# Denominators of 352 channels inverted by GpSimd as a power of minus one

## The chip, the cores and the metric

One core of a Trainium2 chip. The time is device microseconds from launch to end of one execution; where several runs were made, their median is given.

## The reference, cut to what matters

The input is 8 x 1024 tokens of 256 numbers. The first layer is an attention inside each token: its 16 heads have 64 channels, and channel q of a head attends to the channels k up to q of the same head, with one number each for query, key and value.

```python
Q = (x @ Wq + bq).reshape(b, s, H, C) * inv_sqrt_c      # H = 16, C = 64
K = (x @ Wk + bk).reshape(b, s, H, C)
V = (x @ Wv + bv).reshape(b, s, H, C)
scores = jnp.einsum('bshq,bshk->bshqk', Q, K)
scores = jnp.where(mask, -inf, scores)                  # k > q is masked
w = jax.nn.softmax(scores, axis=-1)
attn = jnp.einsum('bshqk,bshk->bshq', w, V).reshape(b, s, H * C)
x = _layernorm(x + attn @ Wo + bo)
```

So each token has 1024 sums of exponentials (denominators) and 1024 weighted sums (numerators), one pair for each channel. The rest of the reference is a second layer (attention over 8 tokens, then a mixture of eight experts) and is not touched by the change.

## The kernel before, in words

`phase_a` computes the first attention, `phase_b` and `phase_c` the second layer. `phase_a` works in 64 tiles of 128 tokens (t) and in each through eight parts (c = 0 to 7); a part is four heads of 64 tokens. The order of the work is written out by hand (`tc.manual_schedule()`): the loop over t and c at the end of `phase_a` calls the steps of a part, and the lists `fill_a`, `middle`, `between` and `fill_b` say which other steps go between them. A sign says for which tile: "" this one, "+" the next, "-" the one before. Each engine executes its instructions in the order in which this loop issued them; an instruction that waits holds up all that is behind it on its engine.

The channels have two ways. Of the 1024 channels, columns 0 to 351 and 672 to 1023 go wholly through TensorE. For the 320 columns between them (`own`), part of the pairs is computed on the token layout by VectorE, GpSimd and ScalarE (`token_scores` L583, `token_less` L591, `token_exp`, `token_weigh` L607 and L616, `token_sums` L625) and added by `complete` (L631, L637).

The TensorE way, for each part:

- `build` (L394, L400) copies queries and keys into the layouts R and L by DMA: four copies of R and two of L are issued by GpSimd, the other copies of L by SP. There are two sets of R and L, used in turn, each for two parts.
- `gather` (L408) is a memset of one number on GpSimd that waits for these copies; the matmuls of the scores wait for it.
- `scores` (L433, L443) makes the scores in PSUM, and ScalarE their exponentials (L458).
- `sums` (L481) makes numerators and denominators, and ScalarE copies them to S (L502). There are two buffers of S, one for the even and one for the odd pair of parts.
- `bring_back` (L521, L522), once for two parts, copies them from S to `nd`, by five DMAs that GpSimd issues. `nd` is [128 tokens, 2, 1024]: numerators and denominators. There is one buffer of it for all tiles.

After the last part of a tile its `nd` is divided while the next tile runs: `invert` (L644) makes reciprocals of the denominators, `divide` (L648) multiplies them with the numerators, both in three pieces of columns: 0 is 0 to 351, 1 is the 320 in the middle, 2 is 672 to 1023. `turn` (L657) transposes the result, `output` (L686) multiplies it by Wo, and `norm_scalars` and `normal` make the layer norm; `norm_scalars` (L76, L79) adds the epsilon to the variance and raises it to the power -0.5 on GpSimd, one column at a time.

Around the change the steps are as follows. `bring_back` of the parts c = 0 and 1 is called at c = 3 (`fill_a`), of c = 2 and 3 at c = 4 (`fill_b`), that of the others as soon as they are done. It overwrites the `nd` of the tile before, so that the steps that read it are issued first: `invert` 0 and 2 at c = 0, `complete` at c = 1, `invert` 1 and the three `divide` at c = 2. At c = 3 and 4 the projections of the next tile's query and value (L355, L322) also go through one PSUM bank (`ps`), which VectorE empties (L356, L329); `products` (L377, L378) are two multiplications on GpSimd, at c = 2 and c = 4, behind VectorE's work (`behind`).

Of the kernel before, what the change touches and what calls it, by code (L numbers as in the profile page):

```python
# [24 lines left out]
FP = mybir.dt.float32  # L25
# [4 lines left out]
ALU = mybir.AluOpType  # L30
# [3 lines left out]
P = 128  # L34
# [18 lines left out]
def fused_kernel(ctx: ExitStack, tc: tile.TileContext, a: dict, out: bass.AP):  # L53
# [68 lines left out]
    ]  # L122

    phase_a(tc, a, ident, x1_d, norm_scalars, share, view)

    late = ctx.enter_context(tc.tile_pool(name="late", bufs=1))
# [39 lines left out]
def phase_a(tc, a, ident, x1_d, norm_scalars, share, view):  # L166
# [8 lines left out]
    nc = tc.nc  # L175
    G = 4
    NR = 4
    T0, TC = 352, 320
# [24 lines left out]
    with (  # L203
# [83 lines left out]
        event = wp.tile([1, 1], FP, name="event")  # L287
        wait = mybir.DependencyInfo(mybir.DependencyClass.Sync, mybir.DependencyReason.DATA)
        nd = wp.tile([P, 2, HID], FP, name="nd")
        Ss = [wp.tile([P, 4, 2 * G, C1], FP, name=f"S{i}") for i in range(2)]  # L290
        nc.gpsimd.memset(Ss[0][:, :, 2 * G - 2 :, 0:32], 0.0)
        nc.gpsimd.memset(Ss[1][:, :, :3, 0:32], 0.0)
# [3 lines left out]
        state = {}  # L296
# [330 lines left out]
        columns = (slice(0, T0), own, slice(T0 + TC, HID))  # L627
# [10 lines left out]
                )  # L638

        def invert(t, n):  # L640
            if n == 0:
                state["att", t] = op.tile([P, HID], FP, name="att")
            cols = columns[n]
            nc.vector.reciprocal(state["att", t][:, cols], nd[:, 1, cols])  # L644

        def divide(t, n):
# [149 lines left out]
        def lead_v(k):  # L796
            xT = view["xT"].rearrange("p c b l n -> p c b (l n)")
            ps = pq.tile([P, 2, 512], FP, name="pair")
            for b in range(2):
# [40 lines left out]
        fill_a = {  # L840
            0: [("", spread_v, 1, 0), ("", spread_v, 1, 1)],
            2: [("-", residual)],
            3: [("", bring_back)],
            5: [
                ("+", maxima, 1), ("", token_weigh, "D"), ("+", token_scores, "F"),
                ("", token_less, "C"), ("-", residual_bias),
# [10 lines left out]
        fill_b = {  # L857
            0: [
                ("", token_less, "F"), ("", token_less, "B"),
                ("-", invert, 0), ("-", invert, 2), ("+", extrema, 0),  # L860
            ],
            1: [("-", complete), ("", token_weigh, "A"), ("", token_scores, "D")],
            2: [
                ("+", products, 0), ("", token_less, "D"),
                ("-", invert, 1), ("", token_sums, "A"), ("-", divide, 0), ("-", divide, 1), ("-", divide, 2),
            ],
            3: [("", token_scores, "C"), ("+", maxima, 0), ("+", extrema, 1), ("", token_weigh, "F")],
            4: [
                ("-", turn), ("+", products, 1), ("", bring_back),
                ("", token_sums, "F"), ("", token_weigh, "B"),  # L870
# [924 lines left out]
```

## Time and profile before

| | |
|---|---|
| median of 2 runs | 4562.82 us (4562.46 to 4563.17) |
| profiled execution, its own time | 4519.66 us |
| its span (first to last instruction) | 4517.9 us |
| clock granted to TensorE, mean | 0.981 |
| TensorE, matmuls | 4306.8 us busy, 95% |
| TensorE, weight loads (beside matmuls) | 2921.1 us, 65% |
| VectorE | 3884.2 us, 86% |
| ScalarE | 3511.9 us, 78% |
| GpSimd | 2958.0 us, 65% |
| `phase_a` | to about 3,800 us of the span |
| reciprocals, L644 | 192 on VectorE, 430.1 us in all |

The page names the engines PE (TensorE; PEld its weight loads), DVE (VectorE), ACT (ScalarE), POOL (GpSimd) and SP. Busy shares are over the whole span. Durations and positions come from the one profiled execution, whose time is 43.2 us (0.9%) below the median of the runs. In a group's line the number after x is the count of instructions, then busy us and mean ns of one, then the idle time of the engine before them and what ended it. In a timeline a line begins with start and duration in us; like instructions in a row are put together. Spans on GpSimd are rough.

### The profile page before, as it was taken

How to read it: one execution, taken by the hardware profiler on the slowest of the kernel's cores; microseconds unless marked ns; L12 is line 12 of the kernel's file. 1: busy time of each engine (PE TensorE's matmuls, PEld its weight loads, DVE VectorE, ACT ScalarE, POOL GpSimd, SP SyncE). 2: the span in 40 equal slices, each digit the busy share in tenths (PEclk: the TensorE clock that was granted, in tenths of full speed). 3: DMA queues.
4: the chain of work that ended last, by engine and by line, in shares of the span. 5: the costliest groups of instructions: out<-in, count | busy, mean ns of one | idle time of the engine just before them, and what ended most of it. 6: DMA issues, size and time to landing. Idle time of an engine off the chain costs nothing. (4 is left out here: it accounts for less than half of the span.)

```text
span 4517.9 us, 164489 instructions
## 1 busy us (share of the span) xinstructions
PE 4306.8 (95%) x68440; PEld 2921.1 (65%) x68440; DVE 3884.2 (86%) x6686; ACT 3511.9 (78%) x5271; POOL 2958.0 (65%) x4391
## 2 busy tenths in 40 slices
PE   7999999999999999999999999999999997888695
PEld 4666666666666666666666666666666665555473
DVE  6889888998888888988998889888888884677778
ACT  5888888888888888888888888888888884444244
POOL 6777777777777777777777777777777772233456
PEclk9999999999999999999999999999999998999897
DMA  2222222222222222222222222222222222232553
GB/s 83 52 54 56 53 54 53 56 54 56 54 53 56 55 56 54 55 55 55 53 56 52 55 54 56 54 56 52 55 55 56 55 53 76 53 76 73 144 167 113
DMA packets 449603, 285.64 MB, mean 63 GB/s; under 512 B 324314, under 2 KB 390234, under 8 KB 448854
## 3 DMA queue, kind: packets, MB, share of 16 engines
q0 software_dynamic: 102368, 164.18, 13.3%
q1 hardware_dynamic: 343718, 109.03, 12.0%
q8 instruction: 536, 8.78, 0.8%
q10 hardware_dynamic: 2768, 1.91, 0.2%
q14 instruction: 213, 1.74, 0.1%
HBM read 72.84 MB, written 33.85 MB: 24 GB/s over the span
## 5 line engine op out<-in xcount | busy, mean ns | idle before, releaser
L458 ACT ACTIVATE e<-pair 128x1024 f32<-128x1024 f32 (+1 forms) x2560 | 2377.1, 983 | 462.2 <-PE pair L443 444.5
L443 PE MATMUL pair<-R,L 32*128 32x128 f32 (+1 forms) x27648 | 1375.4, 321 | 11.9 <-ACT e L458 9.5
L481 PE MATMUL sum<-e,V 128*32 128x256 f32 (+1 forms) x27648 | 1270.5, 320 | 12.2 <-ACT S L502 4.0
L443 PEld LDWEIGHTS pair<-R,L 32*128 32x128 f32 x27648 | 1059.4, 186 | 172.2 <-issue 123.7
L481 PEld LDWEIGHTS sum<-e,V 128*32 128x32 f32 x27648 | 747.4, 110 | 523.0 <-ACT e L458 116.4
L591 POOL TENSOR_TENSOR s<-s,qm 128x1280 f32<-128x1280 f32 (+2 forms) x320 | 596.2, 1888 | 208.6 <-DVE s L583 124.6
L521 POOL DMA_DIRECT2D nd<-S x1024 | 513.9, 509 | 275.2 <-ACT S L502 274.7
L344 DVE COPY V<-vT 32x128 f32<-32x128 f32 (+2 forms) x2048 | 450.9, 220 | 188.9 <-PE sum L481 162.8
L394 POOL DMA_DIRECT2D R<-qm x1024 | 519.6, 522 | 100.5 <-PE pair L443 89.3
L502 ACT COPY S<-sum 128x512 f32<-128x512 f32 (+2 forms) x1152 | 545.8, 488 | 10.6 <-PE sum L481 4.4
L377 POOL TENSOR_TENSOR qm<-qm 128x512 f32<-128x512 f32 x128 | 162.7, 1271 | 487.0 <-DVE qm L356 401.7
L644 DVE RECIPROCAL att<-nd 128x352 f32<-128x352 f32 (+1 forms) x192 | 430.1, 2264 | 1.6 <-DMA nd<-S 1.4
L433 PE MATMUL pair<-late,sel 32*128 32x256 bf16 (+2 forms) x5120 | 385.6, 286 | 3.6 <-ACT e L458 3.6
L616 DVE TENSOR_TENSOR s<-s,vt 128x1280 f32<-128x1280 f32 (+2 forms) x320 | 363.9, 1152 | 6.6
L607 DVE TENSOR_REDUCE part<-s 128x80 f32<-128x1280 f32 (+3 forms) x320 | 358.9, 1137 | 10.2 <-ACT s L598 10.2
L583 DVE TENSOR_TENSOR s<-k,qm 128x1280 f32<-128x1280 f32 (+2 forms) x320 | 363.6, 1153 | 0.1
L625 DVE TENSOR_REDUCE part<-s 128x80 f32<-128x1280 f32 (+3 forms) x320 | 357.5, 1132 | 2.2
L400 POOL DMA_DIRECT2D L<-k x511 | 332.7, 660 | 7.1 <-issue 6.8
L598 ACT ACTIVATE s<-s 128x1280 f32<-128x1280 f32 (+1 forms) x256 | 312.7, 1221 | 8.4 <-POOL s L591 8.4
L76 POOL TENSOR_SCALAR ve<-mv 128x1 f32<-128x1 f32 x128 | 101.5, 793 | 326.5 <-DVE mv L74 300.6
L322 PEld LDWEIGHTS ps<-xT,wv 128*128 128x128 f32 x2048 | 238.3, 192 | 44.3 <-issue 41.8
L433 PEld LDWEIGHTS <-sel 32*128 32x128 bf16 x5120 | 136.2, 92 | 202.1 <-issue 191.8
(259 smaller groups left out, 5708.1 us busy)
## 6 DMA issues: line engine op xcount, KB each, us to landing
R<-qm POOLq DMA_DIRECT2D x1024, 64.0 KB, 2.4
L<-k SPq DMA_DIRECT2D x3577, 8.0 KB
nd<-S POOLq DMA_DIRECT2D x1024, 32.0 KB, 2.0
nd<-S POOLq DMA_DIRECT2D x256, 128.0 KB, 2.6
rows_d<-yx SPq DMA_DIRECT2D x32, 512.0 KB
xT<-in_xT SPq DMA_DIRECT2D x64, 128.0 KB
xr<-in_x SPq DMA_DIRECT2D x64, 128.0 KB
x_d<-x1o SPq DMA_DIRECT2D x64, 128.0 KB
```

Source lines behind the costliest of these rows:

```text
L344: nc.vector.tensor_copy(V[32 * aa : 32 * aa + 32, :, :, aa, 0:4], src[32 * qd : 32 * qd + 32, :n, ww, :, aa, :],)
L394: moved.append((None, nc.gpsimd.dma_start(R[:, b, b, :], q[:, b, :, cols])))
L433: nc.tensor.matmul(bank[u][:, a0:a1].rearrange("p (n i) -> p n i", i=n)[:, :, 0:32], sel[pr].rearrange("p a j -> p (a j)"), late[pr, None, ...
L443: one = nc.tensor.matmul(bank[u][:, starts[h] : starts[h] + 4 * m].rearrange("p (b i) -> p b i", i=m), Lt[pr, 2 * (h0 + h) + jb].rearrange ...
L458: nc.scalar.activation(es[i][:, :, :at], pair[i][:, :, :at], AF.Exp)
L481: nc.tensor.matmul(dst[32 * u : 32 * u + 32, :, width - n :], Vs[ww][:, H1 * jb + v, u, :], e[u // 2][:, u % 2, starts[h] : starts[h] + 4 ...
L502: nc.scalar.copy(S[:, :, to + x : to + x + nh, C1 - width :].rearrange("p b h i -> p h b i"), ps[:, start : start + 4 * nh * width].rearra ...
L521: nc.gpsimd.dma_start(tok[:, b, 0, cols], Sx[:, b, b, :])
L583: shared(nc.vector.tensor_tensor(s, k, q, ALU.mult))
L591: one = nc.gpsimd.tensor_tensor(s, s, m, ALU.subtract)
L616: shared(nc.vector.tensor_tensor(to, s, v, ALU.mult))
L644: nc.vector.reciprocal(state["att", t][:, cols], nd[:, 1, cols])
```

## The change

The reciprocals of columns 0 to 351 (`invert` 0) are made on GpSimd, as the denominators raised to a power that is a constant column of minus one, broadcast over 352 columns. They are issued at c = 3 (`fill_a`) instead of c = 0. The pieces 1 and 2 stay reciprocals on VectorE, where they were. `divide` 0 moves from c = 2 to the start of `fill_b` at c = 3, and the `bring_back` that stood at c = 3 in `fill_a` now follows it.

```diff
         nd = wp.tile([P, 2, HID], FP, name="nd")
+        minus_one = wp.tile([P, 1], FP, name="minus_one")
+        nc.gpsimd.memset(minus_one, -1.0)
...
         def invert(t, n):
+            cols = columns[n]
             if n == 0:
+                nc.gpsimd.tensor_tensor(
+                    state["att", t][:, cols], nd[:, 1, cols], minus_one.to_broadcast([P, T0]), ALU.pow
+                )
+                return
+            if n == 2:
                 state["att", t] = op.tile([P, HID], FP, name="att")
-            cols = columns[n]
             nc.vector.reciprocal(state["att", t][:, cols], nd[:, 1, cols])
...
         fill_a = {
...
-            3: [("", bring_back)],
+            3: [("-", invert, 0)],
...
         fill_b = {
             0: [
                 ("", token_less, "F"), ("", token_less, "B"),
-                ("-", invert, 0), ("-", invert, 2), ("+", extrema, 0),
+                ("-", invert, 2), ("+", extrema, 0),
             ],
...
             2: [
                 ("+", products, 0), ("", token_less, "D"),
-                ("-", invert, 1), ("", token_sums, "A"), ("-", divide, 0), ("-", divide, 1), ("-", divide, 2),
+                ("-", invert, 1), ("", token_sums, "A"), ("-", divide, 1), ("-", divide, 2),
             ],
-            3: [("", token_scores, "C"), ("+", maxima, 0), ("+", extrema, 1), ("", token_weigh, "F")],
+            3: [("-", divide, 0), ("", bring_back), ("", token_scores, "C"), ("+", maxima, 0), ("+", extrema, 1), ("", token_weigh, "F")],
```

## The prediction

> **What bounds the kernel now.** I read the page first, then busy time in stretches, then the timelines of one tile. The first attention takes some 33 of the 40 slices and TensorE's digit there is 9:
>
> ```profile
> PE   7999999999999999999999999999999997888695
> ...
> DVE  6889888998888888988998889888888884677778
> ...
> POOL 6777777777777777777777777777777772233456
> ```
>
> and in busy time by stretches this is one of 800 us (us busy, number of instructions):
>
> ```profile
> 1900.00:2700.00 800.00, 798.30 (x14059) 538.75 (x14060) 719.90 (x1149) 690.15 (x936) 570.74 (x852) 1.00 0.24 55
> ```
>
> That is TensorE busy 798.30, its weight loads 538.75, VectorE 719.90, ScalarE 690.15, GpSimd 570.74, clock 1.00. TensorE sets the pace and lacks only 1.70 us in 800. VectorE is busy for 90%, yet relieving it shortens nothing by itself. GpSimd has 29% free: the projection in a product (L377) starts at 2002.28 and at 2060.51, so a tile takes 58.23 us, of which GpSimd is busy for 41.5 and idle for 16.7.
>
> Then the tile into which the edit falls. GpSimd, then VectorE, then TensorE, one view each (start, duration):
>
> ```profile
> 2048.29 1.27 POOL L377 TENSOR_TENSOR qm<-qm 128x512 f32<-128x512 f32 x1 [6.06 <-DVE qm L356]
> ...
> 2052.07 0.09 POOL L408 MEMSET event<- 1x1 f32 x1
> 2053.47 2.02 POOL L521 DMA_DIRECT2D nd<-S  x4 [1.32 <-ACT S L502]
> 2055.48 0.54 POOL L522 DMA_DIRECT2D nd<-S  x1
> 2055.99 2.02 POOL L394 DMA_DIRECT2D R<-qm  x4
> 2058.01 1.30 POOL L400 DMA_DIRECT2D L<-k  x2
> 2060.51 1.27 POOL L377 TENSOR_TENSOR qm<-qm 128x512 f32<-128x512 f32 x1 [1.21 <-DVE s L616]
> ...
> 2065.51 0.09 POOL L408 MEMSET event<- 1x1 f32 x1
> ```
> ```profile
> 2047.52 0.68 DVE L356 SCALAR_TENSOR_TENSOR qm<-ps,bias 128x512 f32<-128x512 f32 x1
> ...
> 2051.53 1.81 DVE L648 TENSOR_TENSOR att<-att,nd 128x352 f32<-128x352 f32 x3
> 2053.26 0.68 DVE L356 SCALAR_TENSOR_TENSOR qm<-ps,bias 128x512 f32<-128x512 f32 x1
> 2053.87 1.47 DVE L583 TENSOR_TENSOR s<-k,qm 128x1280 f32<-128x1280 f32 x1
> ```
> ```profile
> 2058.07 2.05 PE L322 MATMUL ps<-xT,wv 128*128 128x128 f32 x16
> ...
> 2069.10 0.73 PE L443 MATMUL pair<-R,L 32*128 32x128 f32 x16
> ```
>
> The memset L408 at 2065.51 is what releases the scores of part c = 6, which TensorE starts at 2069.10: this operand is 3.5 us ahead. The one at 2052.07 belongs to c = 4.
>
> **The change part by part.**
>
> *Removed.* One of the two 352-wide reciprocals per tile. Groups by form give the prices (instructions | busy us, mean ns):
>
> ```profile
> L644 DVE RECIPROCAL att<-nd 128x352 f32<-128x352 f32 x128 | 293.0, 2324 | 1.6 <-DMA nd<-S 1.4
> ...
> L591 POOL TENSOR_TENSOR V<-V,qm 128x320 f32<-128x320 f32 x64 | 55.8, 872 | 0.0
> ```
>
> and the view of the tile ve those of GpSimd's one-column operations (ns, least/median/most):
>
> ```profile
> L76 POOL TENSOR_SCALAR ve<-mv x128: 212/362/1372, 160.5 to 4276.2; 128x1 f32<-128x1 f32 x128
> L79 POOL TENSOR_TENSOR rs<-ve,mhalf x128: 555/567/1570, 161.9 to 4276.5; 128x1 f32<-128x1 f32 x128
> ```
>
> 64 x 2.324 = 149 us leave VectorE. None of it stood on the path (TensorE's 1.70 us in 800 bound the gain to about 8 us in the 3,700 of this stage). It brings one thing forward: TensorE ended the projection before L356 at 2045.27 (2043.29 + 1.98), VectorE came to it at 2047.52, so 2.25 of the 2.32 us pull L356 and the GpSimd work behind it ahead, and the memset of 2052.07 ends at 2049.9 instead of 2052.16.
>
> *Added.* A power on 128x352 on GpSimd, 64 times, issued behind that memset. Call its time X. The trace has a power on a single column only, L79, 0.567 us; a plain one-column operation, L76, takes 0.212 at least. So 0.355 us are the power itself, for one column. Nothing shows whether columns overlap.
> Lower end: a plain operation at this width, between 0.872 (320 columns) and 1.361 (640 columns in the same groups), some 0.95 us. Upper end: no overlap, 0.212 + 352 x 0.355 = 125 us. If the power overlapped its columns as well as the plain operation does (0.95 for 352 columns against 0.212 for one, a factor of 4.5), X would be 0.567 x 4.5 = 2.5 us. [...] Between 2.5 and 125 I take the middle by ratio, X = 17.8 us (50 ns a column).
>
> *Moved: the five copies nd<-S (L521, L522) of c = 1.* They stood at c = 3 ahead of all else; now they overwrite what the power and the first multiplication (divide 0) read, and are issued behind both. So the queue reads: power, wait for VectorE's divide 0, five copies, the six operand copies of build 3 (L394, L400), the two products, five more copies, the memset for c = 6. SP's own twelve copies of build 3 wait for none of this. VectorE's queue: divide 0 now stands behind the second L356 and waits for the power; behind it in order are the products of level C (L583), maximum, two scans, level F and the eviction of V (L329).
>
> *How much X is hidden.* With the power from 2049.9: divide 0 ends at 2050.4 + X (0.49 us, the shorter form of L648). The five copies take 2.55, build 3 takes 3.31: GpSimd is free at 2056.3 + X. The products wait for VectorE's L616, which in the trace ends 6.6 us after L583 starts (2053.87 to 2060.43): 2057.0 + X. From the products to the end of the memset the trace has 5.09 us (2060.51 to 2065.60): 2062.1 + X. TensorE wants it at 2069.10, so **7.0 us of X are hidden**. The other routes come later: the copies must have landed (2.0 us) before ScalarE writes S again at 2063.08, 2055.0 + X, hides 8.1; the transposes of att at 2062.58 need divide 0, which hides 12. If VectorE's lead of 2.25 us did not reach GpSimd, 4.7 would be hidden. What is over delays TensorE one for one, since the next tile's power stands behind L377, which waits for VectorE's L356 and that for TensorE (6.06 us of idle above): no slack carries over. Cover gone altogether, the price would be 64 X.
>
> *The port.* The trace shows GpSimd and VectorE stopping one another: L76 takes 1.372 where it starts 0.18 us into VectorE's 1.46 us L583 at 2023.94, and the first L648 of 2051.53 takes some 0.98, against 0.49, while L591 runs until 2052.12. The Trainium skill, "SBUF — State Buffer", section "Who interferes with whom", says that a VectorE instruction with two SBUF inputs and a GpSimd instruction that reads SBUF block each other for the whole instruction, by order of issue. This speaks against the change: a power of many us would hold the port throughout. By that rule the third multiplication would be held until 2049.9 + X and L356 would end at 2051.1 + X; TensorE needs its bank at 2058.07, so again 7.0 would be hidden and the sum would stay. Without it the sum is the one here, since VectorE stands at divide 0 anyway.
>
> *Sum.* 64 x (17.8 - 7.0) = 691 us. The profiled execution has 4519.66 us (span 4517.9); 4519.7 + 691 = 5211. The median of the runs, 4562.82, is 43.2 above it, so the forecast for the median is **5254 us**, 15% slower. One memset of one column ahead of the tiles costs nothing measurable.
>
> **The rivals.**
> *The power is cheap and hidden (not slower).* X below 8.4 us (7.0 + 2% of 4563 / 64) keeps the time within 2%; at 2.5 us it is 4563. For it: GpSimd's 16.7 idle us a tile, and the factor of 4.5 above. Against it: only 7.0 of them can be used at this place, because the largest gap (6.06) lies before the power and waits for TensorE's projection.
> *No overlap.* X = 125: 4563 + 64 x 118 = 12,100 us; GpSimd becomes the engine that sets the tile. For it: 0.355 us for a single column. Against it: plain operations do overlap their columns.
> *VectorE was the bound after all (faster).* 149 us fewer give 4414. Its 90% speak for it, TensorE's 798.30 of 800 against it, and X would have to be under 7.0 too.
>
> **How the numbers follow.** Forecast, X from 8.4 to 45 us: 0.56. Hidden: 0.25. X above 45, up to no overlap: 0.18. Faster by over 2%: 0.01. The time is that of the forecast, 5254. The range starts at 4540, where the hidden case lies, and ends at 7000 (7.0 + 2437 / 64 = 45 us), which leaves the no-overlap case out. Without the hidden case the forecast's own range is 4654 to 7000. About 2% is what a measurement tells from no change here; by that bound: faster 0.01, same 0.25, slower 0.74.
>
> **What would show it.** In the profile after, the 128x352 power's row gives X at once; the loss must be 64 x (X - 7.0), within 64 x 2.3. The second reciprocal must be gone, VectorE's busy time down by 149 us. If X is over 7, TensorE's L443 or its weight load must wait for the memset L408, VectorE's divide 0 for the power, and TensorE's share must fall. X far from 18, or a loss that doesn't follow from X, would make the prediction wrong; so would TensorE waiting for VectorE's L356 or L329 first.

## The result, and the profile after

The changed kernel takes 8041.78 us (8038.67 to 8044.89, two runs) against 4562.82: a ratio of 1.7625, 95% interval 1.7549 to 1.77. It is slower, as forecast, but by 3479 us where 691 were forecast, and outside the range.

The page of the changed kernel, whose span is 8036.9 us: parts 1 and 2, then the group of the power, of VectorE's multiplications and of TensorE's transposes, with the idle time before each and what ended it.

```profile
PE 4550.6 (57%) x68440; PEld 3065.2 (38%) x68440; DVE 3849.0 (48%) x6622; ACT 3507.2 (44%) x5271; POOL 6591.5 (82%) x4456
...
PE   5565455655565455654566455654556555646875
...
POOL 7888888888888888888888888888888888873335
...
L645 POOL TENSOR_TENSOR att<-nd,minus_one 128x352 f32<-128x352 f32 x64 | 3626.8, 56669 | 7.5 <-PE pair L788 7.5
...
L655 DVE TENSOR_TENSOR att<-att,nd 128x352 f32<-128x352 f32 (+1 forms) x192 | 156.4, 840 | 3502.3 <-POOL att L645 3502.2
L664 PE MATMUL pair<-ident,att 128*128 128x128 f32 x512 | 124.2, 424 | 3008.5 <-DVE att L655 3008.5
```

The power takes 56.67 us, 0.161 a column. VectorE waits 3502 us for it, TensorE 3009 us for VectorE. One tile in time, GpSimd first, then VectorE, then TensorE (the line numbers of all changed kernels are a few higher than in the kernel before):

```profile
4070.43 0.09 POOL L410 MEMSET event<- 1x1 f32 x1
4070.48 56.67 POOL L645 TENSOR_TENSOR att<-nd,minus_one 128x352 f32<-128x352 f32 x1
4128.29 2.06 POOL L523 DMA_DIRECT2D nd<-S  x4 [1.13 <-issue]
```
```profile
4071.77 0.68 DVE L358 SCALAR_TENSOR_TENSOR qm<-ps,bias 128x512 f32<-128x512 f32 x1
4127.19 0.53 DVE L655 TENSOR_TENSOR att<-att,nd 128x352 f32<-128x352 f32 x1 [54.74 <-POOL att L645]
```
```profile
4079.52 1.51 PE L483 MATMUL sum<-e,V 128*32 128x256 f32 x32
4127.86 1.94 PE L664 MATMUL pair<-ident,att 128*128 128x128 f32 x8 [46.83 <-DVE att L655]
```

VectorE stands at divide 0 from 4072.45, TensorE 8.6 us later at the transposes. The tile, from one divide 0 to the next (4014.76 to 4127.19), lasts 112.43 us instead of 58.23.

### The profile page after: what moved, and what is told of

Read it like the earlier page. It is cut to its first block, busy times and chain, and to the rows that moved or that the text cites. A ratio compares the mean times of both kernels' runs of the same rounds, so it can differ in the third digit from the quotient of the medians.

```text
span 8036.9 us, 164426 instructions
## 1 busy us (share of the span) xinstructions
PE 4550.6 (57%) x68440; PEld 3065.2 (38%) x68440; DVE 3849.0 (48%) x6622; ACT 3507.2 (44%) x5271; POOL 6591.5 (82%) x4456
## 5 line engine op out<-in xcount | busy, mean ns | idle before, releaser
L645 POOL TENSOR_TENSOR att<-nd,minus_one 128x352 f32<-128x352 f32 x64 | 3626.8, 56669 | 7.5 <-PE pair L788 7.5
L655 DVE TENSOR_TENSOR att<-att,nd 128x352 f32<-128x352 f32 (+1 forms) x192 | 156.4, 840 | 3502.3 <-POOL att L645 3502.2
L664 PE MATMUL pair<-ident,att 128*128 128x128 f32 x512 | 124.2, 424 | 3008.5 <-DVE att L655 3008.5
L483 PE MATMUL sum<-e,V 128*32 128x256 f32 (+1 forms) x27648 | 1352.9, 335 | 245.4 <-ACT S L504 124.1
L445 PE MATMUL pair<-R,L 32*128 32x128 f32 (+1 forms) x27648 | 1452.3, 334 | 16.0 <-ACT e L460 9.5
L664 PEld LDWEIGHTS pair<-ident,att 128*128 128x128 f32 x512 | 100.4, 224 | 3024.4 <-issue 3024.4
L445 PEld LDWEIGHTS pair<-R,L 32*128 32x128 f32 x27648 | 1122.2, 197 | 196.7 <-issue 134.2
L483 PEld LDWEIGHTS sum<-e,V 128*32 128x32 f32 x27648 | 777.9, 114 | 808.9 <-ACT S L504 184.7
L346 DVE COPY V<-vT 32x128 f32<-32x128 f32 (+2 forms) x2048 | 510.6, 249 | 178.9 <-PE sum L483 152.9
L651 DVE RECIPROCAL att<-nd 128x352 f32<-128x352 f32 (+1 forms) x128 | 287.7, 2248 | 136.3 <-DMA nd<-S 136.3
```

The source lines that it names most:

```text
L346: nc.vector.tensor_copy(V[32 * aa : 32 * aa + 32, :, :, aa, 0:4], src[32 * qd : 32 * qd + 32, :n, ww, :, aa, :],)
L445: one = nc.tensor.matmul(bank[u][:, starts[h] : starts[h] + 4 * m].rearrange("p (b i) -> p b i", i=m), Lt[pr, 2 * (h0 + h) + jb].rearrange ...
L483: nc.tensor.matmul(dst[32 * u : 32 * u + 32, :, width - n :], Vs[ww][:, H1 * jb + v, u, :], e[u // 2][:, u % 2, starts[h] : starts[h] + 4 ...
L645: nc.gpsimd.tensor_tensor(state["att", t][:, cols], nd[:, 1, cols], minus_one.to_broadcast([P, T0]), ALU.pow)
```

## The experiments

The times stand beside runs of the kernel before on the same chip: a median of 4559 us for the unread powers of 32 and 64 columns, of 4520 us for all others. Each kernel's own time is a median of 4 or 10 runs; the two with 64 columns, the unread power of 344 columns and the exponent plus one ran once, so they have no interval. "Lost per tile" is the difference divided by 64; "hidden" is the added time less that.

### The new order without the power

```diff
-                    state["att", t][:, cols], nd[:, 1, cols], minus_one.to_broadcast([P, T0]), ALU.pow
+                    state["att", t][:, cols], nd[:, 1, cols], minus_one.to_broadcast([P, T0]), ALU.mult
```

> The changed kernel with the power replaced by a multiplication by minus one on GpSimd, same place, same 352 columns, same operands; it leaves the inversion of these columns out. What is left is the new order alone: one VectorE reciprocal fewer, divide 0 and the copies nd<-S later. If the price of the power is the whole cause, the GpSimd instruction takes about 0.95 us and the time is that of the kernel before, 4563 us within 0.5%. If the new order itself costs (divide 0 or the copies come too late for TensorE), it is above 4563 by 64 times what each tile loses: 1 us per tile would be 4627. If VectorE had been the bound, it is below: down to 4414. The profile should also tell whether the 2.3 us that VectorE saves bring its Q addition (L358) forward: then GpSimd's wait in front of the products, 6.1 us before, falls to about 3.9.

4517.98 us, ratio 0.9992 (0.9983 to 1.0002). The multiplication takes 0.98 us. The new order with one reciprocal fewer per tile costs nothing and brings nothing: TensorE is as busy as before (798.29 us of 800). The waits in the tiles between 300 and 3600 us of the span (us in total, times, longest), of the kernel before and then of this one:

```profile
POOL qm L377 <- DVE qm L356: 358.5, 57, 6.6
...
ACT vt L549 <- DVE r L691: 44.2, 57, 0.9
```
```profile
POOL qm L379 <- DVE qm L358: 358.6, 57, 6.6
...
DVE att L651 <- DMA nd<-S: 112.1, 56, 2.5
...
ACT vt L551 <- DVE r L698: 50.7, 57, 0.9
```

GpSimd's wait for VectorE's L358 (L356 before) has not shortened. The line of L651 shows where VectorE's lead went: the reciprocal that is left (piece 2) now waits 2.0 us a tile for the copies nd<-S of the last parts, for which the removed one left time.

### Fewer columns of power

```diff
-                    state["att", t][:, cols], nd[:, 1, cols], minus_one.to_broadcast([P, T0]), ALU.pow
+                    state["att", t][:, :32], nd[:, 1, :32], minus_one.to_broadcast([P, 32]), ALU.pow
...
             nc.vector.reciprocal(state["att", t][:, cols], nd[:, 1, cols])
+            if n == 2:
+                nc.vector.reciprocal(state["att", t][:, 32:T0], nd[:, 1, 32:T0])
```

With 32 columns:

> The changed kernel with the power on 32 columns; the other 320 of the first piece go back to VectorE's reciprocal at c = 0. By the rate of the changed kernel (56.67 us for 352 columns, 0.567 for one: 0.160 us a column) the power takes 5.5 us. Theory A (the copies and the operands behind the power become late once more than 4.7 us have to be hidden, since VectorE's lead doesn't reach GpSimd): 64 x 0.8 = 53 us more, 4616. Theory B (7.0 us are hidden, as predicted): 4563. If the power has a large fixed part instead of a price per column, it takes far more than 5.5 us.

With 64 columns (64 in place of 32 above):

> The same with 64 columns: the power takes 10.6 us by the rate of the changed kernel. Theory A (4.7 us hidden): 64 x 5.9 = 380 us more, 4943. Theory B (7.0 hidden): 64 x 3.6 = 233 more, 4796. Theory C (9.8 hidden: TensorE stops only at its transposes of att, as in the changed kernel's trace): 64 x 0.8 = 53 more, 4616. TensorE is hardly idle here, so its clock should stay near 1.00 in the tiles; if it falls, the loss of clock doesn't need the long wait.

The power itself, with 32 and with 64 columns (ns, least/median/most):

```profile
L645 POOL TENSOR_TENSOR att<-nd,minus_one x64: 5450/5667/5685, 134.3 to 4083.6; 128x32 f32<-128x32 f32 x64
L645 POOL TENSOR_TENSOR att<-nd,minus_one x64: 10560/10775/10793, 131.6 to 4378.0; 128x64 f32<-128x64 f32 x64
```

It takes 5.67 us for 32 columns and 10.78 for 64 (medians), so the price expected of it was right: 0.16 us a column and some 0.4 to start. Every theory of what is hidden was wrong. With 32 columns: 4820.34 us, ratio 1.0654 (1.0636 to 1.0671), 4.7 us lost per tile and 1.0 hidden; with 64: 5117.79, 9.3 lost and 1.4 hidden. The waits of the run with 32 columns:

```profile
DVE att L657 <- POOL att L645: 221.9, 52, 4.3
...
ACT vt L551 <- DVE r L700: 167.2, 52, 3.4
...
PE sum L483 <- ACT vt L546: 103.2, 52, 2.2
...
PE pair L445 <- POOL event L410: 61.1, 50, 1.5
...
PE sum L483 <- ACT S L504: 19.6, 39, 2.0
```

The memset for c = 6 is late by 1.2 us a tile, a little more than the 1.0 that theory A gives for a power of 5.67 us. The larger loss is one that the prediction doesn't have: VectorE stands 4.3 us at divide 0 and is still late four parts on, when it adds the residual (L700, c = 7). ScalarE copies from the same PSUM bank only after that (L551), and TensorE waits for ScalarE's next copy (L546). In the kernel before ScalarE already waited 0.8 us a tile there: the line "ACT vt L549 <- DVE r L691" above, which I didn't read for what it says: VectorE has no lead at c = 7.

TensorE's clock didn't stay near 1.00 with 64 columns either. It was 0.96 in stretches of 800 us in the tiles, though TensorE never waited longer than 4.2 us, so that some of the clock is lost without a long wait.

### A power that nobody waits for

```diff
+        unread = wp.tile([P, T0 - 8], FP, name="unread")
...
+        def unread_power(t):
+            nc.gpsimd.tensor_tensor(unread, nd[:, 1, : T0 - 8], minus_one.to_broadcast([P, T0 - 8]), ALU.pow)
...
-            3: [("", bring_back)],
+            3: [("-", unread_power), ("", bring_back)],
```

With 344 columns:

> The kernel before, with all its reciprocals on VectorE, and besides a power on 344 columns of the denominators into a tile that nothing reads, issued by GpSimd at c = 3 ahead of the copies nd<-S (344 and not 352 for want of room). No engine waits for its result; only GpSimd's queue stands for 55.4 us. If the queue is the cause, the loss stays: 55.4 less 5.8 hidden by the lead of the memset for c = 6, 64 x 49.6 = 3170 more, some 7700 to 7950 with a lower clock of TensorE. If the cause was VectorE's wait at divide 0, the time falls towards that of GpSimd's busy time alone: 41.5 + 55.4 = 97 us a tile, some 7050. For the port: if a power holds the port against VectorE's instructions with two inputs in SBUF, the products of level C (1.47 us before) last until the power's end, some 50 us; if not, VectorE runs on for several instructions until it needs GpSimd's products.

7733.01 us, 3213 more, 50.2 lost per tile of 55.45 us of power: 5.2 hidden, where 5.8 was expected. So holding GpSimd's queue is enough for nearly the whole loss at this width. TensorE stops in another place, for S, which the late copies free ("PE sum L484 <- ACT S L505", 48 us a tile).

The timeline of this run during the power, GpSimd and then VectorE, answers the question of the port:

```profile
4036.07 55.45 POOL L650 TENSOR_TENSOR unread<-nd,minus_one 128x344 f32<-128x344 f32 x1
```
```profile
4038.39 1.48 DVE L586 TENSOR_TENSOR s<-k,qm 128x1280 f32<-128x1280 f32 x1
...
4043.74 1.21 DVE L619 TENSOR_TENSOR s<-s,vt 128x640 f32<-128x640 f32 x2
...
4048.10 1.49 DVE L619 TENSOR_TENSOR s<-s,vt 128x1280 f32<-128x1280 f32 x1
4099.90 0.69 DVE L386 TENSOR_TENSOR qm<-qm,lo 128x512 f32<-128x512 f32 x1 [50.31 <-POOL lo L381]
```

VectorE's multiplications with two inputs in SBUF run at their usual length (1.47, 1.21 and 1.49 us before) in the midst of the power, and VectorE stops only for a product that stands behind it in GpSimd's queue. So the power does not hold the port for its whole length.

With 32 and 64 columns (32 or 64 in place of T0 - 8):

> As the unread power of 344 columns, with 32: GpSimd's queue at c = 3 stands for 5.7 us, and VectorE waits for nothing new. With 344 columns the loss was 50.2 us a tile for 55.45 us of power, so 5.2 were hidden. If what costs is VectorE standing (theory D), and GpSimd's queue alone only from 5.2 us on, 64 x 0.5 = 30 us are lost, 4550. If GpSimd's queue is what costs in the run with 32 columns that VectorE waited for, the loss is that one's, 4820.

> The same with 64 columns: GpSimd's queue stands for 10.8 us. Theory D with 5.2 hidden: 64 x 5.6 = 358 lost, 4878. Without VectorE's wait making a difference: 5118, as with the 64 columns that VectorE waited for.

4630.46 us for 32 columns, ratio 1.0158 (1.0141 to 1.0175), 1.1 lost per tile and 4.6 hidden; 4900.02 for 64, 5.3 lost and 5.5 hidden. GpSimd's queue alone therefore hides some 5 us at all three widths, and the same power costs 4.7 instead of 1.1 us where VectorE waits for it.

At its start the power does hold the port. VectorE begins the multiplication of the 320 columns in the middle (`divide` 1) 0.3 us after the power (at 4036.38 and 4036.07 us with 344 columns), and this takes the longer the wider the power is. Groups by form (count, busy us, mean ns) of the kernel before, then of the unread powers of 32, 64 and 344 columns:

```profile
L648 DVE TENSOR_TENSOR att<-att,nd 128x320 f32<-128x320 f32 x64 | 30.6, 479 | 0.0
L654 DVE TENSOR_TENSOR att<-att,nd 128x320 f32<-128x320 f32 x64 | 33.4, 521 | 0.0
L654 DVE TENSOR_TENSOR att<-att,nd 128x320 f32<-128x320 f32 x64 | 36.7, 573 | 0.0
L654 DVE TENSOR_TENSOR att<-att,nd 128x320 f32<-128x320 f32 x64 | 65.7, 1026 | 0.0
```

That is some 1.6 ns per column of the power, against its price of 160 ns. With 352 columns, two of VectorE's multiplications fall to the start, beside the power in the changed kernel and beside the plain multiplication of 0.98 us in the first experiment:

```profile
4069.91 1.94 DVE L655 TENSOR_TENSOR att<-att,nd 128x320 f32<-128x320 f32 x2
```
```profile
2052.39 1.94 DVE L655 TENSOR_TENSOR att<-att,nd 128x320 f32<-128x320 f32 x2
```

They take the same time, where the same two take 1.40 beside the power of 32 columns that VectorE waited for (2024.78 there). So the port is held about as long as by the plain multiplication, not for 56.67 us.

### VectorE held, GpSimd not

```diff
+        def unread_reciprocals(t):
+            for _ in range(2):
+                nc.vector.reciprocal(unread, wo.rearrange("p c d -> p (c d)")[:, : T0 - 8])
...
-            3: [("", token_scores, "C"),
+            3: [("-", unread_reciprocals), ("", token_scores, "C"),
```

> The kernel before, with two more reciprocals of 344 columns of a weight on VectorE at the start of c = 3's last steps (where divide 0 stands in the changed kernel), into a tile that nothing reads: VectorE is held for about 4.5 us, as it is for 4.3 in the run with 32 columns of power, and GpSimd has no new work. Theory D (VectorE is what is late: up to the addition of the residual, for which ScalarE already waits 0.8 us, it has 1.8 us of idle time to catch up): 4.5 - 1.8 = 2.7 us lost per tile, 64 x 2.7 = 173 more, 4690; up to 4820, as with the power, if the rest of the loss comes from VectorE too. Rival (TensorE is the bound and VectorE has 5.9 us of idle time in a tile, so that 4.5 are hidden): 4520.

4721.28 us, ratio 1.044 (1.0422 to 1.0457): 3.15 us lost per tile of the 4.62 that the two take, 1.5 hidden. The waits:

```profile
ACT vt L550 <- DVE r L696: 174.0, 53, 3.5
...
PE sum L482 <- ACT vt L545: 108.9, 53, 2.2
...
PE pair L444 <- POOL event L409: 50.9, 54, 1.0
```

These are the waits of the run with 32 columns, without a power. VectorE, 10% idle over a tile, has 1.5 us to spare between c = 3 and c = 7, and its lateness also makes GpSimd's memset late, by way of the products that wait for L617.

And the reciprocal of the 352 columns on VectorE again, in the new order:

```diff
-                nc.gpsimd.tensor_tensor(
-                    state["att", t][:, cols], nd[:, 1, cols], minus_one.to_broadcast([P, T0]), ALU.pow
-                )
+                nc.vector.reciprocal(state["att", t][:, cols], nd[:, 1, cols])
```

> The changed kernel with the 352 reciprocals made by VectorE again, but in the new order (at c = 3, divide 0 and the copies behind them): GpSimd makes no power. VectorE has the same work as before, 2.3 us of it later in the tile. Theory D: 2.3 us more between c = 3 and the addition of the residual, against 1.8 us of idle time, 0.5 us lost per tile: 4550, 0.7% more. Rival (VectorE's place of work doesn't matter while TensorE sets the pace): 4520.

4578.11 us, ratio 1.0124 (1.0108 to 1.0141): 0.9 lost per tile of 2.34 moved, 1.4 hidden. The same slack of 1.4 to 1.5 us from a move of work that VectorE had anyway. Two of its waits:

```profile
POOL nd L523 <- issue: 250.8, 56, 4.6
...
PE sum L483 <- ACT vt L546: 43.2, 56, 1.0
```

GpSimd stands 4.5 us a tile ahead of the copies nd<-S, which are behind divide 0 in the new order, and TensorE has no wait for the memset here. It waits only for vt, 0.8 us a tile. So 4.5 us of GpSimd's queue at this place are hidden, which agrees with the 4.6 of the unread power of 32 columns.

### The power where GpSimd is idle

```diff
+        def power(t):
+            nc.gpsimd.tensor_tensor(
+                state["att", t][:, :32], nd[:, 1, :32], minus_one.to_broadcast([P, 32]), ALU.pow
+            )
...
-            2: [("-", residual)],
+            2: [("-", residual), ("-", power)],
```

Here `invert` 0 stays on VectorE at c = 0, for columns 32 to 351.

> The kernel before with 32 of the first 352 reciprocals made as a power on GpSimd, but issued at c = 2, ahead of the products, where GpSimd is idle for 6.1 us in every tile; divide 0 and the copies nd<-S stay where they were. The power takes 5.7 us as at c = 3. If the place decides (VectorE stands at divide 0 and is late for the rest of the tile), nothing is lost here: 4520 within 0.5%, and GpSimd's idle time ahead of the products falls from 6.1 to about 0.4. If the power costs wherever it stands, it is 4820 as at c = 3. If it held the port against VectorE, VectorE's additions to nd (0.49 and 0.82 us each), which fall into this stretch, would take up to 5.7 us and the time would rise by 64 x 2 to 5 us, 4650 to 4840.

4522.14 us, ratio 1.0003 (0.9993 to 1.0013). GpSimd and VectorE in one tile:

```profile
2041.71 5.51 POOL L651 TENSOR_TENSOR att<-nd,minus_one 128x32 f32<-128x32 f32 x1
2047.73 1.27 POOL L379 TENSOR_TENSOR qm<-qm 128x512 f32<-128x512 f32 x1 [0.52 <-DVE qm L358]
```
```profile
2040.88 2.60 DVE L639 TENSOR_TENSOR nd<-nd,part 128x320 f32<-128x320 f32 x5
```

The 6.1 us of idle time are filled, 0.5 are left, and VectorE's five additions beside the power take 2.60 us as before. The same 32 columns cost 300 us at c = 3 and nothing here, but there is room for no more than these, and nothing is won.

### Another exponent

```diff
-        nc.gpsimd.memset(minus_one, -1.0)
+        nc.gpsimd.memset(minus_one, 1.0)
```

> The changed kernel with the exponent plus one instead of minus one, which leaves the inversion out. If the price is that of the operation whatever the exponent, the power takes 56.7 us again and the time is 4.520 + 3.48 ms, about 8000 us. If it depends on the exponent (a shorter way for some values), the power is shorter and the time falls with it, one for one.

8004.62 us, 54.5 lost per tile, and the power takes 56.68 us again (median), with plus one as with minus one.

## Why the prediction was wrong, point by point

**The price of the power: the term that failed first.** Between 2.5 and 125 us I took the middle by ratio, 17.8, for which no row spoke; it is 56.67. The measured line through 32, 64, 344 and 352 columns is some 0.41 + 0.16 us per column, and it meets L79 (0.567 for one). So of the 0.355 us by which L79 exceeds a plain one-column operation, 0.16 are the price of a column and the rest is paid once. The sum of the upper end, 125 us, counted that part 352 times. Against it the power is shorter by a factor of 2.2, not of 7; whether columns overlap within it, these runs do not tell. The price explains 64 x (56.67 - 17.8) = 2488 us of the 2788 by which the forecast was short. X lay above the 45 us that I gave as the forecast's end, in the rival "no overlap", which had 0.18 and a price twice too high.

**What is hidden.** 7.0 us were to be hidden; by the measured loss it is 56.67 - 54.4 = 2.3. This is the other 300 us (64 x 4.7). Two steps failed, and a third term, the clock below, was missing. VectorE's lead of 2.25 us did not reach GpSimd: it went into a wait for copies (the plain multiplication shows it). And I followed VectorE's queue behind divide 0 only as far as the eviction of V (L329) and the transposes, not to the residual at c = 7 (L691), where it has 1.5 us to spare.

**Where TensorE stops.** I had it wait for the memset L408. At 32 columns it does, for 1.2 us beside 2.0 us for ScalarE's copies of vt. In the changed kernel it comes to the transposes first. Its waits there (300 to 7000 us, 60 tiles):

```profile
PE pair L664 <- DVE att L655: 2810.2, 60, 46.9
...
PE sum L483 <- ACT S L504: 114.9, 60, 3.4
...
PE sum L483 <- ACT vt L546: 110.7, 60, 2.2
```

The route by the transposes hides 56.67 - 46.83 = 9.8 us, the 12 of the prediction less the 2.25 of the lead, and what lies behind it adds 1.9 us a tile for S and 1.8 for vt. These three waits make 50.6 of the 54.4 us.

**The rest: TensorE's clock.** Stretches of the changed kernel: running, waiting, the first 8 us after the wait; and 800 us over several tiles.

```profile
4060.00:4080.00 20.00, 20.00 (x356) 12.89 (x351) 12.28 (x15) 18.11 (x26) 13.43 (x7) 1.00 0.09 19
4085.00:4125.00 40.00, 0.00 (x0) 0.00 (x0) 0.00 (x0) 0.00 (x0) 40.00 (x1) 0.50 0.00 0
4127.00:4135.00 8.00, 4.83 (x60) 3.87 (x64) 7.81 (x11) 1.72 (x3) 6.70 (x13) 0.71 0.24 69
...
3000.00:3800.00 800.00, 440.05 (x7234) 296.15 (x7238) 373.18 (x594) 354.46 (x481) 698.25 (x456) 0.77 0.11 29
```

The granted clock (third figure from the end) is 1.00, then 0.50 while TensorE waits, then 0.71. The same eight transposes take 1.94 us (4127.86, above) against 1.09 before:

```profile
2062.58 1.09 PE L657 MATMUL pair<-ident,att 128*128 128x128 f32 x8
```

In a tile TensorE is busy for 440.05 x 112.43 / 800 = 61.8 us against 58.1, so 3.7 us of the loss are slower matmuls; with the waits this makes 54.3 of 54.4. The prediction has no such term. The same sum closes elsewhere: over the whole span TensorE is busy 1.2 us a tile longer than before with 32 columns (4386.3 us in all against 4306.8) and 2.3 with the unread power of 344 (4452.0), and with its waits, 3.5 and 47.9, this makes the 4.7 and the 50.2 lost.

The Trainium skill, "TensorE: Matmul & The Clock Gate", Part 1, gives half the clock for the first 3.4 us or so of sustained work after idling; the trace agrees on the half, but the slow stretch is longer here: after the one wait of the unread power of 344 columns the matmuls are slow for some 5 us (2.79, 1.92 and 2.23 us for groups that take 1.51, 1.04 and 2.05).

**The port.** The skill's rule ("SBUF — State Buffer", "Who interferes with whom") doesn't hold for the length of this instruction: a GpSimd operation that reads SBUF is to block VectorE's two-input operations for its whole length. Here it blocked one of them at its start, 1.03 us instead of 0.48 beside 344 columns, and after that they ran at normal length during the power. For short operations before the change the trace had shown the blocking. The sum didn't rest on it.

**What was right.** TensorE is the bound and relieving VectorE brings nothing (0.9992). The new order with one reciprocal fewer costs nothing; with the reciprocal kept on VectorE it costs 0.9 us a tile. GpSimd's queue alone, as worked out ahead of the unread power, hides about 5 us (4.6 to 5.5 measured, 5.8 worked out). What is over is lost one for one: from 64 to 352 columns the power grows by 45.9 us and the loss by 45.0.

**What stays open.** In the run with 32 columns VectorE's wait (4.3 less 1.5) and GpSimd's queue (1.1, and 1.1 us more idle between the power and the copies, which wait for divide 0) add to 5.0, and 4.7 are measured: these two overlap in a way that wasn't tried apart. Why TensorE's matmuls slow down there and hardly where VectorE alone is held (4322.5 us busy), with waits as long, isn't shown. Why the port comes free while the power goes on wasn't tried either.

## What to carry to other kernels

The price of one column says little about 352: measure an unknown operation at two widths, or bound it by the whole single-column time, before moving it to an engine that others wait for. When a change holds an engine, follow that engine's queue to the end of the period and look in the waits for the place where someone already waits for it, however little; its idle share over the period is no slack. Idle time counts only where it lies: the same power was free in GpSimd's gap and cost 4.7 us a tile ten microseconds later.

## What the runs showed of the hardware

GpSimd's power in float32 takes 0.16 us per column of 128 partitions beside some 0.4 us to start, for exponents of -1 and +1 alike, whereas a multiplication of 352 columns takes 0.98 us in all. VectorE's operations with two SBUF inputs are held up by it at its start only: one of 320 columns that began 0.3 us after a power of 344 columns took 1.03 us instead of 0.48, later ones the usual time. TensorE's granted clock was 0.50 from 4 us into a wait of 47 us to its end, and matmuls just after it took up to 1.8 times as long (2.73 us against 1.51 for 32 matmuls of 128x256).
